# Four steps of h in a row, then x Wx of two pairs: regrouping a recurrent layer on one core of a Trainium2

## The chip, the cores and the metric

The kernel runs on one core of a Trainium2 chip. The metric is the time of the device in microseconds for one execution of the whole program. The engines are called as in the profile: PE is TensorE's matmul and PEld its weight load, DVE is VectorE, ACT is ScalarE, POOL is GpSimd, SP is SyncE, from which nearly all transfers are issued.

## The reference

There are 64 sequences of 256 steps with 1024 features. The first layer is a recurrence over the 256 steps; the second multiplies by a gate that depends on the sequence alone.

```python
def step(prev_h, xw):
    next_h = jnp.tanh(prev_h @ Wh + xw)
    return (next_h, next_h)
xW = jnp.einsum('ntd,dh->nth', x, Wx) + b
...
_, h_t = jax.lax.scan(step, h0, xW_t)
x = x + jnp.swapaxes(h_t, 0, 1)
...
h = jax.nn.silu(q_pool @ W1.T + b1)
gate = jax.nn.sigmoid(h @ W2.T + b2)[:, None, :]
...
return v + a
x = x + _L1_cond_ref(x, cond_1024, W1, b1, W2, b2)
```

The Haar transform is linear and the gate is the same for all its levels, so its result is v times the gate. With v + a and the outer addition, the second layer becomes a multiplication of (x + h) by a factor 2 + gate.

## The kernel before, in words

**Steps and pairs.** Two steps are a pair (S = 2), so there are 128 pairs (NP); x of a pair is one slab of 128 x 1024 in fp32, step and sequence interleaved in its free dimension. Six slabs exist. The product x Wx doesn't depend on h and is made for a whole pair; the product of h has to wait for the step before.

**The product of h.** A step multiplies h (64 x 1024) by Wh in full fp32 with one level of Strassen's scheme: seven half-size products (`strassen_product`, L190), each of 16 matmuls in the code, 32 matmuls and 32 weight loads in the trace. Their order in the loop is 1, 4, 2, 5, 6, 7, 3. The four quarters of h are finished as their products come in: DVE adds (L710, L725, L731), ACT takes the tanh (L685), DVE transposes the quarter to hT (L689). L720 adds two operands that both lie in SBUF. After the last quarter, DVE makes four sums of quarters for the next step (`strassen_sides`, L225 to L228). ACT puts the next step's x Wx in three PSUM banks, into which products of h accumulate (`put_part`, L607; called by `put_next`).

**The product of x.** x is split into a high and a low part[...]: x0 (the high bits, cast by ACT, L309), x1 (x - high, L298), and x2, a combination of both for the mixed terms (L303). `XWork.whole` (L331) issues 16 mixed matmuls, then 16 main ones with x1 and 16 with x0. `take_mixed` evacuates the mixed product with ACT and adds b with POOL (L319, L320); `finish_half` adds the main product with DVE (L374). The sum of a pair goes to DRAM and comes back as two tiles by step (`store` L384, `reload` L392, eight transfers). The tiles high, x0, x1, x2 and sum have one buffer each; xw has three.

**The loop.** From step ALONE = 12 on, the order on all engines is that of the program. Each pair of steps is followed by `beside_x`: the product of x for the pair two ahead (`now`), the addition of h to both steps of x by POOL (L645), the multiplication by the factor by POOL (`scale`, L494), the split of the pair three ahead (`nxt`), and the store of the finished pair. PE thus runs two steps of h (14 products), one pair of x (48 matmuls of 128 x 512), two steps of h, and so on. Steps before 12 are made with other code that the change hardly touches; they leave five pairs in DRAM (`kept`) that are multiplied by the factor later. The last x product comes after step 251; steps 252 to 255 follow each other without one. The last step is stored in a layout of its own (`times_factor`, `plus_x`).

**SP's queue.** Within `beside_x` it holds the store of the last sum (made to wait for `mark`, the copy of u in the step, so that transfers keep out of the products of h), the load of a slab, the reloads of that sum, and the store of the slab finished one pair earlier.

Of the kernel before, what the change touches and what calls it, by code (L numbers as in the profile page):

```python
# [51 lines left out]
F32 = mybir.dt.float32  # L53
# [16 lines left out]
S = 2  # L70
NP = T // S
# [12 lines left out]
def tile_cond_resid(  # L84
# [197 lines left out]
    class XWork:  # L282
# [17 lines left out]
        def difference(self) -> None:  # L300
            i = self.i
            self.x2 = split.tile([P, D], F32R, tag="x2", name=f"x2_{i}")
            nc.vector.scalar_tensor_tensor(  # L303
                out=self.x2, in0=self.x1[:].bitcast(F32), scalar=-UP, in1=self.high, op0=ALU.mult, op1=ALU.add
            )
# [195 lines left out]
    for t in range(ALONE):  # L501
# [56 lines left out]
        if LATE <= t < LATE + B:  # L558
# [6 lines left out]
            if k == B - 1:  # L565
                factor, factor_n = gate_factor(b2_n), b2_n
# [7 lines left out]
        if s == S - 1:  # L574
            del pairs[i]
            load_x(i + 3)
# [22 lines left out]
    load_x(i + 3)  # L599
# [9 lines left out]

    def not_ahead_of(dma, ins) -> None:  # L610
# [7 lines left out]
    leaving = []  # L618

    def store_y() -> None:  # L620
        while leaving:
            j = leaving.pop()
            nc.sync.dma_start(out=yT[j], in_=pairs.pop(j))

    def transfers(i: int, mark) -> None:

        if mark and i + 1 < NP - 1:
# [4 lines left out]
        if mark and i + 1 < NP - 1:  # L632
            xws[i + 1] = later.reload(d)
        store_y()

    def beside_x(t: int, steps: list, mark):

        i = t // S
        x = pairs[i]
        transfers(i, mark)  # L640
        now = coming
        if now:
            now.whole()
        for r, v in steps:
            nc.gpsimd.tensor_add(of_step(x, r), of_step(x, r), blocks(v))  # L645
# [24 lines left out]
    coming.cast()  # L670
    later, coming = beside_x(t, [(s, hT)], None)
    x_n = None
    for t in range(ALONE, T):
        i, s = divmod(t, S)
        final = t == T - 1
        xw, before = xws[i][s], hT
# [28 lines left out]
        if s == 0 and coming is not None:  # L705
# [11 lines left out]
        put_next(0) if s == 0 else None  # L717
# [4 lines left out]
        put_next(2) if s == 0 else None  # L722
# [41 lines left out]
        if t >= 2 * B and t % 2 == 1 and kept:  # L764
            j, r = divmod((t - 1) // 8 - B // 4, S)

            def at(v):
                return v.rearrange("p (b s n) -> p s b n", b=B, s=S)[:, r]

            if t % 8 == 1:  # L770
                again = const.tile([P, W], F32, tag="spare", name=f"again{t}")
                by_block = again[:].rearrange("p (b n) -> p b n", b=B)
                nc.sync.dma_start(out=by_block, in_=at(kept[j]))
            elif t % 8 == 3:
                v = again[:].rearrange("p (b g m) -> p g b m", b=B, g=G)
                nc.gpsimd.tensor_mul(v, v, blocks(factor))
            elif t % 8 == 5:
                nc.sync.dma_start(out=at(yT[j]), in_=by_block)
                if (j + 1, r + 1) == (len(kept), S):
                    kept = []  # L780
# [34 lines left out]
```

## Time and profile before

| what | value |
| --- | --- |
| median of 3 runs | 3047.43 us (3046.83 to 3047.49) |
| the profiled execution, whole | 3048.26 us |
| its span | 3046.5 us |
| granted clock of PE | 1.00 |
| main matmuls of x, L274 | 4064; 32 in 7.25 us by the chain of waits |
| mixed matmuls of x, L274 | 2032 |
| additions of h to x by POOL, L645 | 243, mean 1389 ns |
| multiplications by the factor by POOL, L494 | 244, mean 1772 ns |
| one such addition by DVE, L748 | 684 ns |
| DVE sum of quarters L226 and L227 | mean 311 and 813 ns |

The durations of matmuls in the profile overlap (a product of h is listed with 32 records of 273 ns and passes in 0.87 us), so they are read from start to start, or from the chain of waits, which lists the pieces of PE's stream one behind the other. In the timeline a bracket behind an instruction gives the idle time of its engine before it and what ended it.

### The profile page before, as it was taken

What the parts mean: (1) busy time and instruction counts of PE and PEld (TensorE: products, weight loads), DVE (VectorE), ACT (ScalarE), POOL (GpSimd) and SP (SyncE); (2) the same over time, 40 slices, a digit from 0 to 9 for tenths busy, and PEclk for the clock granted to TensorE, in tenths of its full rate; (3) what the DMA queues carried; (4) which work ended last, traced back from release to release, by engine and by line L of the source; (5) the groups of instructions that cost most, each with busy time, mean ns of one, the idle gap of its engine ahead of it and who ended that gap; (6) DMA issues with size and microseconds to landing.
All of it is one profiled execution on the core that took longest, in us unless ns stands there. A gap on an engine that the chain in (4) does not pass through costs nothing.

```text
span 3046.5 us, 141663 instructions
## 1 busy us (share of the span) xinstructions
PE 3036.6 (100%) x63862; PEld 2708.3 (89%) x63862; DVE 2028.4 (67%) x4683; ACT 868.6 (29%) x2641; POOL 1176.9 (39%) x766
## 2 busy tenths in 40 slices
PE   9999999999999999999999999999999999999999
PEld 6888899888988998889888998899888988898888
DVE  7566666666666666666666666666666666666666
ACT  3222232222222222222222222232222222222222
POOL 2224433443344433433343334433443334333432
PEclk9999999999999999999999999999999999999999
DMA  7323322332233223222222223222322232222222
GB/s 264 125 82 100 100 93 94 106 101 89 93 104 105 93 89 103 99 86 86 96 95 93 86 91 98 95 86 87 102 96 85 86 101 98 86 89 99 100 85 79
DMA packets 164605, 300.40 MB, mean 99 GB/s; under 512 B 44192, under 2 KB 110496, under 8 KB 164000
## 3 DMA queue, kind: packets, MB, share of 16 engines
q1 hardware_dynamic: 163856, 290.81, 28.7%
q8 instruction: 501, 8.21, 1.1%
q14 instruction: 104, 0.85, 0.1%
q10 hardware_dynamic: 144, 0.52, 0.1%
HBM read 154.93 MB, written 136.31 MB: 96 GB/s over the span
## 4 chain that ended last, share of the span: by engine, by line
PE 99%; POOL 0%; DMA 0%; DVE 0%; issue 0%; SPq 0%; ACT 0%; DVEq 0%; ACTq 0%
PE main L274 30%; PE acc L195 22%; PE mixed L274 16%; PE m_h L195 15%; PE main_h L195 14%; PE m L195 1%; PE acc L212 0%; PE gate_ps L212 0%; POOL sum L320 0%; DMA wx<-wx 0%; PE acc_raw L212 0%; DVE x L298 0%; SPq L406 0%; DVE sum L374 0%; ACT acc L607 0%
## 5 line engine op out<-in xcount | busy, mean ns | idle before, releaser
L645 POOL TENSOR_TENSOR x<-x,hT 128x512 f32<-128x512 f32 x243 | 333.1, 1389 | 1714.4 <-DVE hT L689 1696.5
L274 PE MATMUL main<-wx,x 128*128 128x512 f32 x4064 | 945.7, 389 | 0.8 <-DVE x L298 0.8
L274 PEld LDWEIGHTS main<-wx,x 128*128 128x128 f32 x4064 | 762.1, 188 | 161.6 <-issue 2.2
L274 PE MATMUL mixed<-wx,x 128*128 128x512 f32 x2032 | 499.3, 397 | 0.0
L274 PEld LDWEIGHTS mixed<-wx,x 128*128 128x128 f32 x2032 | 371.8, 188 | 98.0 <-issue 24.8
L685 ACT ACTIVATE h<-h 128x128 f32<-128x128 f32 x976 | 275.6, 306 | 553.2 <-DVE h L710 333.2
L494 POOL TENSOR_TENSOR x<-x,factor 128x512 f32<-128x512 f32 x244 | 427.4, 1772 | 5.8 <-DVE factor L480 5.7
L320 POOL TENSOR_TENSOR sum<-sum,b_row 128x512 f32<-128x512 f32 x254 | 383.5, 1530 | 57.4 <-ACT sum L319 50.4
L298 DVE TENSOR_TENSOR x<-x,x_high 128x1024 fp32r<-128x1024 f32 x127 | 212.3, 1672 | 230.7 <-PE main L274 230.6
L689 DVE STREAM_TRANSPOSE hT<-h 128x128 f32<-128x128 f32 x972 | 297.7, 306 | 38.7 <-ACT h L685 38.5
L710 DVE TENSOR_TENSOR h<-acc,y 128x128 f32<-128x128 f32 x244 | 71.1, 292 | 333.7 <-PE acc L195 333.7
L195 PE MATMUL acc<-wh,s 128*32 128x128 f32 x8160 | 273.9, 273 | 0.0
L195 PE MATMUL acc<-t,hT 128*32 128x128 f32 x8160 | 270.3, 273 | 0.6 <-ACT acc L607 0.4
L195 PE MATMUL acc<-wh,hT 128*32 128x128 f32 x8160 | 270.2, 273 | 0.0
L195 PE MATMUL main_h<-wh,s 128*32 128x128 f32 x7808 | 261.9, 273 | 0.6 <-issue 0.6
L195 PE MATMUL m_h<-t,s 128*32 128x128 f32 x7808 | 261.0, 273 | 0.4 <-issue 0.4
L195 PE MATMUL m_h<-wh,hT 128*32 128x128 f32 x7808 | 261.2, 274 | 0.0
L704 ACT COPY y<-m_h 128x128 f32<-128x128 f32 x244 | 65.1, 267 | 684.5 <-PE m_h L195 669.2
L195 PE MATMUL main_h<-t,s 128*32 128x128 f32 x7808 | 259.4, 273 | 0.1
L607 ACT COPY acc<-xw 128x128 f32<-128x128 f32 x732 | 177.7, 264 | 257.0 <-DMA xw<-sum_d 187.3
L195 PEld LDWEIGHTS m_h<-wh,hT 128*32 128x32 f32 x7808 | 208.6, 110 | 42.8 <-issue 42.8
L319 ACT ACTIVATE sum<-mixed 128x512 f32<-128x512 f32 x254 | 149.8, 598 | 321.6 <-PE mixed L274 215.8
(81 smaller groups left out, 3418.7 us busy)
## 6 DMA issues: line engine op xcount, KB each, us to landing
x<-xT SPq DMA_DIRECT2D x127, 512.0 KB, 5.2
sum_d<-sum SPq DMA_DIRECT2D x127, 512.0 KB, 3.2
xw<-sum_d SPq DMA_DIRECT2D x1016, 64.0 KB, 2.0
yT<-x SPq DMA_DIRECT2D x122, 512.0 KB, 2.7
wh<-wh SPq DMA_DIRECT2D x8, 512.0 KB, 10.8
w<-w1T SPq DMA_DIRECT2D x8, 512.0 KB, 8.7
w<-w2T SPq DMA_DIRECT2D x8, 512.0 KB, 4.2
wx<-wx SPq DMA_DIRECT2D x7, 512.0 KB, 8.7
```

Source lines behind the costliest of these rows:

```text
L195: nc.tensor.matmul(out=out[q * R : (q + 1) * R], lhsT=a[:, k * R : (k + 1) * R], rhs=wh_s.sides[i][k][:, q], start=first and k == 0, stop= ...
L274: nc.tensor.matmul(out=acc[h], lhsT=v[:, k * P : (k + 1) * P], rhs=wx_s[k][which][:, h * HALF : (h + 1) * HALF], start=start and k == 0, s ...
L298: nc.vector.tensor_sub(self.x1, x, self.high)
L319: nc.scalar.activation(s, self.mixed[h], AF.Copy, scale=-DOWN)
L320: nc.gpsimd.tensor_add(s, s, b_row[:, h * HALF : (h + 1) * HALF])
L494: nc.gpsimd.tensor_mul(of_step(x, s), of_step(x, s), blocks(factor))
L607: nc.scalar.copy(part, xws[t // S][t % S][:, j])
L645: nc.gpsimd.tensor_add(of_step(x, r), of_step(x, r), blocks(v))
L685: nc.scalar.activation(quad(h, j), quad(h, j), AF.Tanh)
L689: nc.vector.transpose(quad(hT, j), quad(h, j))
L704: nc.scalar.copy(y[:, 0], m16)
L710: nc.vector.tensor_add(quad(h, 0), accs[0], y[:, 0])
```

## The change

The program works in groups of M = 4 steps. Products of h of four steps follow each other; then `beside_x` issues the products of x for two pairs, `one` (which was split during the x products before) and `two` (split while `one` is multiplied, from the slab loaded one group earlier), and splits a third pair, `three`, for the next group's `one`. x2 is made from high and x instead of from high and x1, with another scale, which `take_mixed` takes into account; so it is made ahead of x1. The addition of h to x is done by DVE in each step (`residual`), right after the sums of quarters, or, for the last step of a group, ahead of the splits. POOL keeps the multiplications by the factor and the addition of b. Four xw tiles are needed by group: the fourth lies in a constant tile that is free by then. `put_next` runs in the first three steps of a group; for the first step of a group, the three banks are filled during the x products. The kept pairs and the last step's x are handled in the same rhythm, and in the last group DVE does the multiplications of the three steps before the last.

```diff
@@ -68,6 +69,7 @@
...
 S = 2
+M = 4
 NP = T // S
@@ -301,7 +303,7 @@
...
             nc.vector.scalar_tensor_tensor(
-                out=self.x2, in0=self.x1[:].bitcast(F32), scalar=-UP, in1=self.high, op0=ALU.mult, op1=ALU.add
+                out=self.x2, in0=self.high, scalar=1.0 + DOWN, in1=pairs[i], op0=ALU.mult, op1=ALU.subtract
             )
@@ -316,7 +318,7 @@
...
                 s = self.sum[:, h * HALF : (h + 1) * HALF]
-                nc.scalar.activation(s, self.mixed[h], AF.Copy, scale=-DOWN)
+                nc.scalar.activation(s, self.mixed[h], AF.Copy, scale=-1.0)
                 nc.gpsimd.tensor_add(s, s, b_row[:, h * HALF : (h + 1) * HALF])
@@ -383,11 +385,16 @@
...
-        def reload(self, d) -> list:
+        def reload(self, d, late: bool = False) -> list:
             d = d[:].rearrange("(s g m) (q f) -> s q m g f", s=S, g=G, q=Q)
...
             for s in range(S):
-                t = xwpool.tile([P, 4, E], F32, tag="xw", name=f"xw{self.i * S + s}")
+                name = f"xw{self.i * S + s}"
+                if late and self.i * S % M + s == M - 1:
+                    t = const.tile([P, 4, E], F32, tag="h0T", name=name)
+                else:
+                    t = xwpool.tile([P, 4, E], F32, tag="xw", name=name)
                 for q in range(Q):
@@ -563,7 +570,7 @@
...
             if k == B - 1:
-                factor, factor_n = gate_factor(b2_n), b2_n
+                factor = gate_factor(b2_n)
         if t + 1 == ALONE:
@@ -573,6 +580,7 @@
...
             del pairs[i]
+        if s == S - 1 or t + 2 == ALONE:
             load_x(i + 3)
@@ -596,7 +604,6 @@
...
     xws = {ALONE // S: xw_next}
-    load_x(i + 3)
@@ -606,6 +613,10 @@
...
         return part
+    def residual(t: int, hT) -> None:
+        v = x_step(t)
+        nc.vector.tensor_add(v, v, blocks(hT))
@@ -615,65 +626,98 @@
...
-    leaving = []
-    def store_y() -> None:
-        while leaving:
-            j = leaving.pop()
-            nc.sync.dma_start(out=yT[j], in_=pairs.pop(j))
-    def transfers(i: int, mark) -> None:
-        if mark and i + 1 < NP - 1:
+    def store_y(i: int) -> None:
+        nc.sync.dma_start(out=yT[i], in_=pairs.pop(i))
+    def beside_x(t: int, mark):
+        i = t // S
+        steps = [(i - 1, 0), (i - 1, 1), (i, 0), (i, 1)] if mark else [(i, 1)]
+        if mark:
             d, dma = later.store()
...
             load_x(i + 4)
-        if mark and i + 1 < NP - 1:
-            xws[i + 1] = later.reload(d)
-        store_y()
-    def beside_x(t: int, steps: list, mark):
-        i = t // S
-        x = pairs[i]
-        transfers(i, mark)
-        now = coming
-        if now:
-            now.whole()
-        for r, v in steps:
-            nc.gpsimd.tensor_add(of_step(x, r), of_step(x, r), blocks(v))
-        if now:
-            now.take_mixed()
-        for r, _ in reversed(steps):
-            scale(x, r)
-        leaving.append(i)
-        nxt = None
+        if mark:
+            xws[i + 1] = later.reload(d, True)
+        one = coming
+        one.whole()
+        residual(t, hT)
+        for j, r in steps[:2]:
+            scale(pairs[j], r)
+        if mark:
+            store_y(i - 1)
+        if i + 5 < NP:
+            load_x(i + 5)
+        elif i + 4 < NP:
+            ends.append(slab("ends"))
+            nc.sync.dma_start(out=ends[0][:, :W], in_=xN)
+        one.take_mixed()
+        if mark:
+            accs[:] = [put_part(t + 1, j) for j in range(3)]
+        two = three = None
         if i + 3 < NP:
-            nxt = XWork(i + 3)
-            nxt.low()
-        if now:
-            now.finish_half(0)
-        if nxt:
-            nxt.difference()
-        if now:
-            now.finish_half(1)
-        if i + 2 >= NP - 1:
-            store_y()
-        if i + 2 == NP - 1:
-            xws[i + 2] = now.relay()
-        return now, nxt
+            two = XWork(i + 3)
+            two.difference()
+            two.low()
+        else:
+            x_n, factor_n = ends[0][:, :W], ends[0][:, W:]
+            nc.vector.transpose(factor_n, factor)
+            nc.vector.tensor_mul(x_n, x_n, factor_n)
+        one.finish_half(0)
+        one.finish_half(1)
+        for j, r in steps[2:]:
+            scale(pairs[j], r)
+        kept_step(t)
+        d, _ = one.store()
+        store_y(i)
+        xws[i + 2] = one.reload(d, True)
+        if two:
+            two.cast()
+            two.whole()
+            two.take_mixed()
+        if i + 4 < NP:
+            three = XWork(i + 4)
+            three.difference()
+            three.low()
+        if two:
+            two.finish_half(0)
+            two.finish_half(1)
+        return two, three
+    again = []
+    def kept_step(t: int) -> None:
+        n, odd = divmod(t // M - ALONE // M, 2)
...
     accs = [put_part(ALONE, j) for j in range(3)]
-    coming = later
+    coming, later, ends = later, None, []
     coming.cast()
-    later, coming = beside_x(t, [(s, hT)], None)
-    x_n = None
+    later, coming = beside_x(t, None)
     for t in range(ALONE, T):
...
         final = t == T - 1
-        xw, before = xws[i][s], hT
+        last_of_group = t % M == M - 1
+        xw = xws[i][s]
         m16, m5, m7 = (bank(tag, f"{tag}_h{t}")[:, :E] for tag in ("m16", "main0", "main1"))
@@ -689,20 +733,19 @@
...
         def put_next(j: int) -> None:
-            if not final:
+            if not last_of_group:
                 nxt[j] = put_part(t + 1, j)
...
         def times_factor(v: slice) -> None:
-            nc.vector.tensor_mul(h[:, v], h[:, v], factor_n[:, v])
+            nc.vector.tensor_mul(h[:, v], h[:, v], ends[0][:, W + v.start : W + v.stop])
         def plus_x(v: slice) -> None:
-            nc.vector.tensor_add(h[:, v], h[:, v], x_n[:, v])
+            nc.vector.tensor_add(h[:, v], h[:, v], ends[0][:, v])
             nc.sync.dma_start(out=yT[i][:, W + v.start : W + v.stop], in_=h[:, v])
...
         nc.scalar.copy(y[:, 0], m16)
-        if s == 0 and coming is not None:
+        if t % M == 0 and coming is not None:
             coming.cast()
@@ -714,12 +757,17 @@
...
             plus_x(slice(0, E))
-        put_next(0) if s == 0 else None
+        elif t > T - M:
+            v = x_step(t - 1)
+            nc.vector.tensor_mul(v, v, blocks(factor)) if t < T - 1 else None
+            store_y(i - 1) if t == T - S else None
+        put_next(0)
         strassen_product(m16, sides[6], 6)
...
         nc.vector.tensor_add(y[:, 2], accs[2], u)
-        put_next(2) if s == 0 else None
+        put_next(2)
         strassen_product(m7, sides[7], 7, True)
@@ -737,47 +785,20 @@
...
         transpose(2)
-        put_next(1) if s == 0 else None
+        put_next(1)
         transpose(1)
         sides = strassen_sides(hT, t)
+        accs = nxt
         if t == T - 2:
...
             last = slab("last")
-            v = of_step(pairs[i], s)
-            nc.vector.tensor_add(v, v, blocks(hT))
-            nc.vector.tensor_mul(blocks(last[:, :W]), v, blocks(factor))
+            residual(t, hT)
+            nc.vector.tensor_mul(blocks(last[:, :W]), x_step(t), blocks(factor))
             nc.sync.dma_start(out=yT[i][:, :W], in_=last[:, :W])
-        if s == 1:
-            later, coming = beside_x(t, [(1, hT), (0, before)], mark)
-            for o in range(3):
-                put_next(o)
-        accs = nxt
-        if t == T - 4 * B - 1:
-            x_n = const.tile([P, W], F32, tag="spare", name="x_n")
-            nc.sync.dma_start(out=x_n, in_=xN)
-        if t == T - 4 * B + 1:
-            nc.vector.tensor_scalar_add(factor_n, factor_n, 2.0)
-            nc.vector.tensor_mul(x_n, x_n, factor_n)
...
+        elif last_of_group:
+            later, coming = beside_x(t, mark)
+        else:
+            residual(t, hT)
```

More of the change, by code (lines that the diff above doesn't have):

```diff
@@ new lines, in beside_x, with at @@
+        return two, three
+    again = []
+    def kept_step(t: int) -> None:
+        n, odd = divmod(t // M - ALONE // M, 2)
+        def at(v, n: int):
+            return v[n // S].rearrange("p (b s n) -> p s b n", b=B, s=S)[:, n % S]
+        if not 0 <= n <= S * len(kept):
+            return
+        if odd and again:
+            v = again[0][:].rearrange("p (b g m) -> p g b m", b=B, g=G)
+            nc.gpsimd.tensor_mul(v, v, blocks(factor))
+        if not odd:
+            if again:
+                v = again.pop()[:].rearrange("p (b n) -> p b n", b=B)
+                nc.sync.dma_start(out=at(yT, n - 1), in_=v)
+            if n < S * len(kept):
+                again.append(const.tile([P, W], F32, tag="spare", name=f"again{n}"))
+                v = again[0][:].rearrange("p (b n) -> p b n", b=B)
+                nc.sync.dma_start(out=v, in_=at(kept, n))
@@ L739, in tile_cond_resid @@
         transpose(2)
-        put_next(1) if s == 0 else None
+        put_next(1)
         transpose(1)
         sides = strassen_sides(hT, t)
+        accs = nxt
         if t == T - 2:
             last = slab("last")
-            v = of_step(pairs[i], s)
-            nc.vector.tensor_add(v, v, blocks(hT))
-            nc.vector.tensor_mul(blocks(last[:, :W]), v, blocks(factor))
+            residual(t, hT)
+            nc.vector.tensor_mul(blocks(last[:, :W]), x_step(t), blocks(factor))
             nc.sync.dma_start(out=yT[i][:, :W], in_=last[:, :W])
-        if s == 1:
-            later, coming = beside_x(t, [(1, hT), (0, before)], mark)
-            for o in range(3):
-                put_next(o)
-        accs = nxt
-        if t == T - 4 * B - 1:
-            x_n = const.tile([P, W], F32, tag="spare", name="x_n")
-            nc.sync.dma_start(out=x_n, in_=xN)
-        if t == T - 4 * B + 1:
-            nc.vector.tensor_scalar_add(factor_n, factor_n, 2.0)
-            nc.vector.tensor_mul(x_n, x_n, factor_n)
[L764 to L780, printed above, removed]
+        elif last_of_group:
+            later, coming = beside_x(t, mark)
+        else:
+            residual(t, hT)
 def kernel(x, cond_1024, L0_cond_Wx, L0_cond_Wh, L0_cond_b, L1_cond_W1, L1_cond_b1, L1_cond_W2, L1_cond_b2):
```

## The prediction

> **What bounds the kernel now.** I read the page first (busy shares, chain, queues), then the chain of waits in windows in the middle of the loop, then the timeline of the same windows, and last the end of the run, where four steps already follow each other without x products between them.
>
> ```profile
> span 3046.5 us, 141663 instructions
> PE 3036.6 (100%) x63862; PEld 2708.3 (89%) x63862; DVE 2028.4 (67%) x4683; ACT 868.6 (29%) x2641; POOL 1176.9 (39%) x766
> ...
> q8 instruction: 501, 8.21, 1.1%
> ...
> PE 99%; POOL 0%; DMA 0%; DVE 0%; issue 0%; SPq 0%; ACT 0%; DVEq 0%; ACTq 0%
> ```
>
> The reader is to see that TensorE's own order sets the end: 99% of the chain is PE. Only three things can move the time: how many products there are (the change leaves them alone), what a switch between kinds of products costs, and gaps on PE. The chain of waits over one pair of steps prices the switch:
>
> ```profile
> 1515.16 0.87 PE m_h L195 x32
> 1516.03 1.75 PE acc L195 x64
> ...
> 1521.27 3.85 PE mixed L274 x16
> 1525.12 7.25 PE main L274 x32
> 1532.38 1.01 PE m_h L195 x32
> 1533.39 1.75 PE acc L195 x64
> ```
>
> A product of h in the stream takes 0.87 us, the first after x 1.01: 0.14 more. 32 matmuls of x take 7.25, so 16 should take 3.63; the first 16 after h take 3.85: 0.22 more. So one h-to-x-to-h pair of switches costs 0.36 us. The step s=1 (from 1515.16) follows s=0 with no gap.
>
> The same chain where it is not smooth:
>
> ```profile
> 738.70 0.61 PE acc L195 x22
> 739.31 0.18 issue
> 739.49 1.39 PE acc L195 x41
> ...
> 743.18 0.28 issue
> 743.47 0.52 PE main_h L195 x10
> ```
>
> Here PE stops in mid-product, waiting for no semaphore ("issue"). I took the starts of all such stops in h from the trace. Before the last four steps there are 19, in 17 of the 120 runs of h products; each ends at the same count of PE records modulo 256 (193 or 194), 2.3 to 2.9 us after the start of the last 16 KB packet on q8 (739.49 after 737.20, 743.47 after 740.65). So they are waits for a page of instructions. They hold the weight loads 0.07 to 0.55 us and lie 7.4 to 12.1 us into a run of h products, none earlier.
>
> The timeline shows what room VectorE has in a step:
>
> ```profile
> 1516.82 0.29 DVE L228 TENSOR_TENSOR s<-hT,s 128x128 f32<-128x128 f32 x1
> 1517.92 0.29 DVE L710 TENSOR_TENSOR h<-acc,y 128x128 f32<-128x128 f32 x1 [0.80 <-PE acc L195]
> 1519.89 0.29 DVE L720 TENSOR_TENSOR y<-y,u 128x128 f32<-128x128 f32 x1 [0.66 <-ACT u L719]
> ...
> 1522.40 2.75 POOL L645 TENSOR_TENSOR x<-x,hT 128x512 f32<-128x512 f32 x2 [14.24 <-DVE hT L689]
> 1522.61 1.38 DVE L227 TENSOR_TENSOR s<-s,hT 128x128 f32<-128x128 f32 x1
> ```
>
> [...] early in a run of h, the packet starts 0.25 of a page (64 of 256 records) earlier against the products than after a stop[...] L227 takes 1.38 us beside L645, and 0.28 elsewhere (739.13)[...].
>
> **The change part by part.**
>
> *Fewer switches.* Before, x products run 121 times (after t = 11, 13 ... 251), each for one pair; after, 61 times (11, 15 ... 251), all but the last for two. 60 pairs of switches go: 60 x 0.36 = **21.6 us off**, all on the chain.
>
> *Longer runs of h.* 120 runs of two steps become 60 of four; the last one of four is there before too. A product is 64 PE records (32 loads, 32 matmuls) in 0.873 us, so a page of 256 lasts 3.49 us. From the packets of q8: within runs of h the next packet starts 3.75 us (121 cases, first to second) and 3.72 us (115, second to third) after the one before, not 3.49; the packet takes 1.10 us, the wait after a stop shows some 1.4 us from landing to use and 1.2 from use of one page to the next packet: 3.7 together. So in a run of h each page loses about 0.26 us, paid from the lead of 64 records = 0.87 us, which x products (0.23 us a matmul, so 96 records in 11.1 us) refill. A run of two steps has 14 x 64 / 256 = 3.5 pages, of which on average 3 have their boundary and their successor inside: 3 x 0.26 = 0.78, under 0.87, so a stop only in some runs. That fits: mean length of the runs 12.43 us, usual 12.36, 0.06 a run. A run of four steps has 7 pages, 6.5 counted so: 6.5 x 0.26 = 1.69, less 0.87, is 0.82; packets scatter (0.9 to 1.45 us) and a run cannot gain below nothing, so I take **0.85 us a run**. Sum: 60 x 0.85 = 51.0, less what the 120 short runs lose now, 120 x 0.06 = 7.4: **43.6 us on**. Bounds: a page at 3.65 us gives 6.5 x 0.16 - 0.87 = 0.17 a run, 2.8 us in all; the seven packets in the last four steps start at 3016.30 to 3040.72, 4.07 us each, or 3.91 without the 0.97 us that PE there waits for data: 6.5 x 0.42 - 0.87 = 1.86 a run, 104 us.
>
> *Residual on VectorE.* 243 additions leave POOL (L645, 1389 ns); the added one is L748's form, 684 ns. In the step it comes after L228 and before L710, where VectorE waits 0.80: it fits with 0.1 to spare, and L710 may be 0.1 late, which its transpose (needed 1.7 us later by the next step's first product) absorbs: 0. Behind it in VectorE's queue wait L710, L712 and the transposes; were that cover gone, 0.3 us a step. In the last step of a group it lies beside x.
>
> *Scaling.* POOL's multiplication of the earlier pair (L494; 1.28 us unhindered at 1528.10) no longer follows POOL's own addition in x. It can start as soon as the residual on VectorE is done, thus inside the second and third step of the group. There it lies between about 2.7 and 4.0 us after the step's start; the next VectorE instruction with two SBUF inputs is L720 at 4.7. Cost 0. If both multiplications come together in one step, the second meets L720; the end of the run shows the price:
>
> ```profile
> 3031.44 2.52 POOL L494 TENSOR_TENSOR x<-x,factor 128x512 f32<-128x512 f32 x2
> ...
> 3032.88 1.22 DVE L720 TENSOR_TENSOR y<-y,u 128x128 f32<-128x128 f32 x1 [0.42 <-ACT u L719]
> ...
> 3034.59 0.38 PEld L195 LDWEIGHTS m_h<-wh,hT 128*32 128x32 f32 x16 [0.16 <-issue]
> 3035.25 0.81 PEld L195 LDWEIGHTS acc<-t,hT 128*32 128x32 f32 x32 [0.28 <-DVE hT L689]
> ```
>
> L720 0.93 late, and PE loses up to 0.44.
>
> *Second split and transfers.* Per x stretch of about 22 us VectorE does two splits (1.56 + 1.45 + 1.67 each) and four finishes (0.68): 12.1 us, in room of 22. x2 now needs high and x alone, so it can follow the mixed products (3.85 us in); x1 follows the main x1 products (7.5 in), x0's cast (1.05 on ACT) the end at 11.1, needed at 18.5. ACT's evacuation of the second pair waits for the first sum's store (done near 12, 3.2 to landing), 15.5, and the addition by POOL is done by 19.5, before VectorE's finish at 20.4. SP's queue holds two stores, two loads, sixteen reloads (0.57 each) and two y stores: the second reload ends near 23, used first two steps later. The load behind the first y store waits for its landing (2.7), with the next 512 KB not needed before the following stretch. No wait of PE: 0.
>
> *The end.* At t = 253 the old order held back the evacuation copies (0.41 of PE), and POOL met L720 (up to 0.44). Both go, though the page waits take part of that back: **0.7 off**.
>
> Sum: 43.6 - 21.6 - 0.7 = +21.3. The profiled execution took 3048.26 (1.76 outside its span); it would take 3069.6. The median of the runs is 0.83 lower: **3069 us**.
>
> **The rivals.** *A, likeliest, 60%:* as worked out, 3053 to 3100. *B, faster, 17%:* the wait for pages in a run of four steps stays near what two short runs lose (0.12 together). Place: boundaries in steps three and four; price: 21.6 and 0.7 off, 3025; at 0.17 a run 3028. It decides below 0.12 + 0.36 = 0.48 us a run. For it: 103 of the 120 short runs have no stop, and transfers in h get rarer. Against it: the packets fall behind steadily, and stops come only late in a run, and the last four steps have three such stops, 11.8, 19.7 and 23.5 us in. *C, balance, 13%:* 0.4 to 0.58 a run, within 0.2% (6 us, about what a measurement of this kernel tells from no change), 3047. *D, slower, 10%:* collisions of POOL's scaling with L720, twice in each group at 0.44: 60 x 0.88 = 53, less 22.3, 3078. Against it is the early start of the scaling; and with PE late for pages, part of it would be hidden.
>
> **How the numbers follow.** Faster is B, 0.17; same C, 0.13; slower A and D, 0.70. Range: A's upper bound with 1.3 us a run gives 60 x 1.3 - 7.4 - 22.3 = +48; D on top of some of A lies near +50; downward half of B's chance must be taken in with C. I take 3035 to 3098; A alone would be 3055 to 3090.
>
> **What would show it.** In the chain of the changed kernel, 1.01 and 3.85 appear once per 28 products: else the first term is wrong. Pieces named "issue" in steps three and four, about 0.85 us a run of four steps (24.6 us without): 0.1 means B. A wait of PE on ACT or DVE at L720's late end means D. L710 after the residual at its old place in the step confirms the cost of nothing for it. The forecast fails if pages arrive every 3.6 us or less in long runs.

## The result, and the profile after

The changed kernel takes 3050.65 us (median of 20 runs, 3044.25 to 3057.76), the kernel before 3046.25 us beside it (20 runs, 3045.17 to 3048.18). The ratio is 1.0015, with a 95% interval from 1.0008 to 1.0022: +4.4 us, small but clear of the noise, where +21.3 us were forecast. The profiled execution took 3049.05 us, 0.8 more than the one before; the analysis below is of this pair, and the other 3.6 us of the medians are in executions without a trace. So this is a large rearrangement that moved the time hardly at all, and the question is where its two large terms went.

The page of the changed kernel, header, queue of instructions and shares of the chain:

```profile
span 3047.2 us, 141801 instructions
...
PE 3029.6 (99%) x63862; PEld 2716.6 (89%) x63862; DVE 1791.4 (59%) x4928; ACT 866.9 (28%) x2641; POOL 808.3 (27%) x521
...
q8 instruction: 501, 8.21, 1.1%
...
PE 99%; issue 0%; POOL 0%; DMA 0%; DVE 0%; SPq 0%; ACT 0%; DVEq 0%
```

PE has the same 63862 matmuls and still makes 99% of the chain; POOL has 245 instructions fewer, DVE 245 more. "issue" rounds to 0% here but now stands right behind PE. PE is busy 7.0 us less in a span that is 0.7 us longer: something was saved, and something else was put in its place.

The chain of waits over one group of four steps and the x products behind it (start, duration, what):

```profile
1663.16 1.01 PE m_h L197 x32
1664.17 1.75 PE acc L197 x64
...
1680.14 0.32 issue
1680.46 0.96 PE main_h L197 x27
...
1688.58 3.85 PE mixed L276 x16
1692.43 7.25 PE main L276 x32
1699.69 3.63 PE mixed L276 x16
1703.32 7.25 PE main L276 x32
1710.57 1.01 PE m_h L197 x32
```

The dear first pieces, 1.01 and 3.85, appear once per 28 products; the second pair of x passes at 3.63, so nothing is lost inside the double stretch. The price is in the middle: PE stops for 0.32 us at 1680.14, 17 us into the run, with no semaphore to wait for.

The stops by engine and tile, from the view of waits (total us, times, longest); after, and below it before:

```profile
PEld m_h L197 <- issue: 29.1, 79, 0.7
...
PEld acc L197 <- issue: 13.0, 32, 1.0
PEld mixed L276 <- issue: 12.9, 65, 0.2
...
PEld main_h L197 <- issue: 6.2, 17, 0.6
```

```profile
PEld m_h L195 <- issue: 44.3, 126, 0.6
...
PEld mixed L274 <- issue: 24.8, 125, 0.2
```

The "mixed" line is the switch to x: 125 times 0.2 before, 65 after. The "m_h" line of before is nearly all the switch back (one per run); after, it mixes that switch with real stops, and "acc" and "main_h", 1.2 and 2.4 us in the view of before, are almost all stops. Taken one by one from the trace, the changed kernel has 88 such stops with 27.6 us in all, in 42 of its 61 runs of h. Every one ends where the count of PE records is 193 or 194 modulo 256, and only 3 of the 88 lie in the first 12 us of a run. I read them as waits for a page of instructions, 256 records to one packet on q8: the 501 packets carry 8.21 MB, 16 KB each, and 501 x 256 is 128,256, 0.4% above the 127,724 records of PE and PEld.

I measured every run of h from its first product to the first x product, and every x stretch likewise, in both traces. A run of four steps without a stop takes 24.59 us (the shortest of the 60 that have x products behind them), one of two steps 12.364.

| where | forecast, us | found, us | how found |
| --- | --- | --- | --- |
| switches | -21.6 | -21.3 | x stretches 1343.8 to 1330.8, and 60 x (24.59 - 2 x 12.364) in h |
| page waits in the runs of h of the loop | +43.6 | +21.9 | 60 runs lose 0.482 us each (28.95), 120 short runs lost 7.08 |
| last four steps | -0.7 | -0.8 | 26.40 to 25.65 us, to the start of the last matmul |
| start of the loop's first x product | 0 | +1.4 | 180.06 to 181.44 us |
| behind the start of the last matmul | 0 | -0.5 | 5.42 to 4.95 us |
| sum, in the span | +21.3 | +0.7 | 3046.5 to 3047.2 |

The same trace ties the loss of a run to its pages. Between the 60 runs, the loss and the mean spacing of the packets on q8 go together (correlation 0.90): the 30 runs with the closest packets (3.60 us on average) lost 0.15 us each, the other 30 (3.79 us) 0.82. A stop may also put off the next packet (in this trace the next one starts 1.2 us behind a stop's end at the median), so this shows the tie and not its direction, for which the places of the stops and the experiments are needed.

### The profile page after: what moved, and what is told of

Its sections match the earlier page's. It is cut to its first block, busy times and chain, and to the rows that moved or that the text cites. A ratio compares the mean times of both kernels' runs of the same rounds, so it can differ in the third digit from the quotient of the medians.

```text
span 3047.2 us, 141801 instructions
## 1 busy us (share of the span) xinstructions
PE 3029.6 (99%) x63862; PEld 2716.6 (89%) x63862; DVE 1791.4 (59%) x4928; ACT 866.9 (28%) x2641; POOL 808.3 (27%) x521
## 3 DMA queue, kind: packets, MB, share of 16 engines
q8 instruction: 501, 8.21, 1.1%
## 4 chain that ended last, share of the span: by engine, by line
PE 99%; issue 0%; POOL 0%; DMA 0%; DVE 0%; SPq 0%; ACT 0%; DVEq 0%
PE main L276 30%; PE acc L197 22%; PE mixed L276 16%; PE m_h L197 14%; PE main_h L197 14%; PE m L197 1%; PE acc L214 0%; PE gate_ps L214 0%; POOL sum L322 0%; DMA wx<-wx 0%; PE acc_raw L214 0%; DVE x L300 0%; SPq L413 0%; ACT sum L321 0%; SPq L119 0%
## 5 line engine op out<-in xcount | busy, mean ns | idle before, releaser
L322 POOL TENSOR_TENSOR sum<-sum,b_row 128x512 f32<-128x512 f32 x254 | 409.9, 1626 | 1119.0 <-ACT sum L321 1109.4
L501 POOL TENSOR_TENSOR x<-x,factor 128x512 f32<-128x512 f32 x242 | 368.2, 1531 | 1007.0 <-issue 561.4
L300 DVE TENSOR_TENSOR x<-x,x_high 128x1024 fp32r<-128x1024 f32 x127 | 176.9, 1393 | 269.8 <-PE main L276 269.7
L376 DVE SCALAR_TENSOR_TENSOR sum<-main,sum 128x512 f32<-128x512 f32 x254 | 175.4, 691 | 203.1 <-PE main L276 181.4
L197 PE MATMUL acc<-wh,s 128*32 128x128 f32 x8160 | 282.6, 273 | 1.3 <-issue 1.0
L197 PE MATMUL acc<-wh,hT 128*32 128x128 f32 x8160 | 279.5, 273 | 1.6 <-issue 1.3
L197 PE MATMUL main_h<-t,s 128*32 128x128 f32 x7808 | 269.2, 273 | 1.2 <-issue 0.8
L305 DVE SCALAR_TENSOR_TENSOR x<-x_high,x 128x1024 fp32r<-128x1024 f32 x127 | 174.5, 1374 | 155.3 <-PE mixed L276 155.2
L197 PEld LDWEIGHTS acc<-wh,s 128*32 128x32 f32 x8160 | 238.0, 110 | 4.3 <-issue 4.1
L197 PEld LDWEIGHTS m_h<-wh,hT 128*32 128x32 f32 x7808 | 217.8, 110 | 26.3 <-issue 25.9
```

Of the source, the lines that this page charges most:

```text
L197: nc.tensor.matmul(out=out[q * R : (q + 1) * R], lhsT=a[:, k * R : (k + 1) * R], rhs=wh_s.sides[i][k][:, q], start=first and k == 0, stop= ...
L300: nc.vector.tensor_sub(self.x1, x, self.high)
L305: nc.vector.scalar_tensor_tensor(out=self.x2, in0=self.high, scalar=1.0 + DOWN, in1=pairs[i], op0=ALU.mult, op1=ALU.subtract)
L376: nc.vector.scalar_tensor_tensor(out=v, in0=self.main[h], scalar=1.0 + DOWN, in1=v, op0=ALU.mult, op1=ALU.add)
L501: nc.gpsimd.tensor_mul(of_step(x, s), of_step(x, s), blocks(factor))
```

## The experiments

Theory P: PE outruns its supply of instructions in a run of h. Each page arrives some 0.2 us later than it is used up (3.69 us from packet to packet, 3.49 for 256 records in the products' time), a lead (0.87 us, the prediction's estimate from the 64 records that it read in the trace of before) covers the first pages, and what a run loses depends on its length and on the spacing of the packets on q8, on no other engine. Rival D: part of the time comes from data (the residual on VectorE, POOL's scaling meeting L768, the old L720). Rival T: the transfers delay the pages, so the losses come from where the DMAs lie. A "ratio" is to the kernel before, with its 95% interval. The runs were made in four groups, each on another chip, so each is compared with the kernel before that ran beside it: 3044.74 us for e1, e3, e4 and e5; 3044.26 for e2, e2b, e4b and e7; 3043.12 for a_after_again, e5c, e8 and e8b; 3043.84 for a_after_third, e2_runs_alone_again and e9.

### The residual alone, and without it

The first of these takes the kernel before and lets VectorE add h to x within the step; the second takes the changed kernel and gives the addition back to POOL.

```diff
-        for r, v in steps:
-            nc.gpsimd.tensor_add(of_step(x, r), of_step(x, r), blocks(v))
+        r, v = steps[0]
+        nc.vector.tensor_add(of_step(x, r), of_step(x, r), blocks(v))
...
+        elif s == 0:
+            v = of_step(pairs[i], s)
+            nc.vector.tensor_add(v, v, blocks(hT))
```

> The kernel before with one part of the change alone: h is added to x by VectorE right after the sums of quarters in each step, no longer by POOL; runs of two steps as before. Theory (pages of instructions and switches decide): PE does not wait for it, within 2 us of the kernel before. Rival (the residual on VectorE delays the steps): 0.1 us a step or more, 24 us slower.

Measured: 3044.31 us (13 runs), ratio 1.0 [0.9992, 1.0008]; runs of two steps 12.397 us on average, x stretches 11.105.

```diff
     def residual(t: int, hT) -> None:
         v = x_step(t)
-        nc.vector.tensor_add(v, v, blocks(hT))
+        (nc.vector if t == T - 2 else nc.gpsimd).tensor_add(v, v, blocks(hT))
```

> The changed kernel with one part undone: h is added to x by POOL (1.3 us) in each step, just before the multiplications by the factor. Theory (pages hold the runs): POOL's instruction meets the sums of quarters and L710 waits behind them; the runs have slack from the late pages, 0 to 10 us slower. Rival (moving the addition to VectorE is what makes long runs possible): over 0.1 us a step, more than 24 us slower.

Measured: 3044.75 us (13 runs), ratio 1.0002 [0.9994, 1.001]; runs 25.045 us, 88 stops with 24.4 us at the page's place in the count of records, none for data. POOL's addition does meet the sums of quarters here (L229 takes 1206 ns on average), and PE still doesn't wait. The unaltered changed kernel did not run on that chip; on three others its mean run was 24.90 to 25.08 us, and within that spread the engine of the residual is worth nothing in either arrangement. So rival D falls. The groups of the changed kernel's profile say the same (operations, then busy us and mean ns, then idle time before):

```profile
L619 DVE TENSOR_TENSOR x<-x,hT 128x512 f32<-128x512 f32 x244 | 167.1, 685 | 0.0
...
L229 DVE TENSOR_TENSOR s<-s,hT 128x128 f32<-128x128 f32 x255 | 75.8, 297 | 0.0
...
L768 DVE TENSOR_TENSOR y<-y,u 128x128 f32<-128x128 f32 x244 | 71.3, 292 | 163.5 <-ACT u L767 163.3
```

L229, the old L227, falls from 813 to 297 ns with POOL's addition gone from beside it, and rises to 1206 where the addition is given back to POOL. L768 at 292 ns shows no meeting with POOL's scaling; the timeline shows how it is avoided:

```profile
1671.28 0.69 DVE L619 TENSOR_TENSOR x<-x,hT 128x512 f32<-128x512 f32 x1
...
1672.10 1.29 POOL L501 TENSOR_TENSOR x<-x,factor 128x512 f32<-128x512 f32 x1 [11.55 <-issue]
...
1672.17 0.29 DVE L753 TENSOR_TENSOR h<-acc,y 128x128 f32<-128x128 f32 x1 [0.20 <-PE acc L197]
...
1674.14 0.29 DVE L768 TENSOR_TENSOR y<-y,u 128x128 f32<-128x128 f32 x1 [0.66 <-ACT u L767]
```

VectorE is through with the residual 0.20 us before L753 may start, and POOL's multiplication ends at 1673.39, 0.75 before L768. L753, beside that multiplication, still takes 0.29: from 180 us on, 120 of its 244 executions overlap an instruction of POOL's, and these take 292 ns on average like the other 124. It has an operand in PSUM; L768 has both in SBUF, and took 1.22 us beside POOL in the prediction's view of the end (there L720).

### PE alone

This kernel computes nothing of the layer: PE issues products of h, in runs of 14 to 56, each behind 48 matmuls in the shape of x's, with no wait on another engine, and at the end runs whose matmuls are twice as wide.

```python
for r in range(14):
    for n in (14, 21, 28, 42, 56):
        x_part()
        for _ in range(n):
            product(m, E)
for r in range(6):
    x_part()
    for _ in range(28):
        product(wide, F)
```

> Nothing of the reference is computed but the products themselves: PE alone issues runs of 14, 21, 28, 42 and 56 products of h's shape, without a wait for any other engine, each behind 48 matmuls of x's shape, 14 times over, and then six runs of 28 products twice as wide. Theory (3.69 us a page against 3.49, lead 0.87): stops a run of 0.05, 0.2, 0.5, 1.1 and 1.8 us, and none in the wide runs, which need a page in 7 us. Rival (data of other engines, or transfers beside the runs): no stops at any length.

> PE alone in runs of 14 to 56 products of h's shape, as before, on the chip of this batch; nothing else of the reference is computed. Theory: a page each 3.60 to 3.70 us in the long runs, as 3.64 before, and stops in runs of 28 of 0.1 to 0.3 us. If this chip has slow pages, the changed kernel's mean run is longer too.

Mean loss of a run above the shortest possible, in us:

| products in the run | 14 | 21 | 28 | 42 | 56 |
| --- | --- | --- | --- | --- | --- |
| first chip | 0.00 | 0.02 | 0.14 | 0.46 | 1.26 |
| another chip | 0.03 | 0.09 | 0.15 | 0.51 | 0.99 |

The packets came every 3.64 and 3.63 us in the long runs, closer than in the kernels here. Waits of the first of the two:

```profile
PEld m L134 <- issue: 53.4, 152, 0.6
...
PEld x L147 <- issue: 14.9, 70, 0.4
...
PEld wide L134 <- issue: 2.1, 6, 0.4
```

With no other engine at work PE still stops (70 of the 152 are the switch), and the loss grows faster than the length of the run, as a lead that is used up would make it. The wide runs have the same number of instructions in twice the time and lose nothing: 48.484 us every time, six waits for six switches. So P's mechanism needs neither data nor transfers. The size was over-expected: for 28 products 0.5 us was expected, while 6.5 pages at 3.64 us, 0.15 above 3.49, less 0.87 of lead give an estimate of 0.11, near the 0.14 found. That is also less than a third of the 0.48 in the changed kernel.

The same with 512 KB loads and stores going on all the while:

```diff
+    for j in range(240):
+        t = slabs.tile([P, D], F32, tag="traffic", bufs=2, name=f"traffic{j}")
+        nc.sync.dma_start(out=t, in_=xT[j % NP])
+        nc.sync.dma_start(out=yT[j % NP], in_=t)
```

> The same runs, with 512 KB loads from and stores to DRAM going on all the time. Theory: the round trip of a page hardly depends on transfers (packets take 1.05 us beside x and 1.10 in h): stops within 30% of those of the quiet runs. Rival (pages are late because of transfers): several times as long.

The transfers ended near 955 us of 3217, which the slices of the page show (busy tenths of the DMA engines, and GB/s):

```profile
DMA  7777777777760000000000000000000000000000
GB/s 279 270 277 266 269 269 269 268 273 268 269 232 4 3 4 3 3 4 3 4 4 3 4 3 3 4 3 4 3 4 3 3 4 3 3 3 2 2 2 9
```

While they went on, runs of 28 lost 1.06 to 3.96 us each; afterwards 0 to 0.2. The packets came every 3.95 us instead of 3.62, although a packet itself took 1.07 us as ever. So my expectation for it (stops within 30% of the quiet ones) failed, and rival T is right for this kernel: with such traffic beside the runs, a page came 0.33 us later. In the changed kernel, transfers beside the runs are not the cause: its traffic lies beside the x products, with about 33 KB in the first 3 us of a run and next to nothing from there to its last 0.6 us. The packets in its runs came every 3.69 us, and the 321 of 333 intervals between them with less than 2 KB of traffic also average 3.69.

### More instructions in the run

Two NoOps ahead of each product of the loop shorten the page in products (3.88 instead of 4).

```diff
     def strassen_product(out, a, i: int, first: bool = False) -> None:
+        for _ in range(nop_now[0]):
+            nc.tensor.nop(hint="pad", nofuse=True)
...
+        nop_now[0] = 2
         strassen_product(m16, sides[1], 1, True)
```

> The changed kernel with two empty instructions (NoOp) on TensorE's queue ahead of each product of h, 56 in a run of four steps (0.22 of a page). Theory (pages arrive every 3.7 us in a run): a run needs 0.22 x 3.69 = 0.8 us more where it is already held by pages, 0.6 to 0.8 on average, so 35 to 50 us slower than the changed kernel (3050.65). Rival (the longer runs wait for data of other engines): no more than a few us.

Measured: 3154.34 us, ratio 1.0357 [1.0343, 1.0371]; runs 26.77 us, 1.69 more than the 25.08 of the changed kernel's first trace, where 0.6 to 0.8 were expected; all 61 runs have stops, about 250 of them at the page's place, with some 110 us; x stretches unchanged at 22.00. The direction is P's, the size is not. The records of NoOps in a row start about 74 ns apart (below), which would be 4.1 us for the 56 of a run, so they may add time of their own as well as records to the page. It supports P but measures nothing cleanly.

### Where the page boundary falls

A group of the changed kernel takes 53 instructions less than eight pages, so the boundary wanders through the runs. With 53 NoOps per group it stays at one place. I put them behind 8 matmuls of the first of the two pairs, and chose with a larger number in the first stretch the boundary 24 records into the run (first kernel), or 128 (second).

```diff
             for h in range(2):
                 for k in range(B):
                     x_matmul(self.mixed, self.x2, 2, h, k, True, True)
+                if h == 0:
+                    for _ in range(53 if self.i % 2 and self.i > 7 else 72 if self.i == 7 else 0):
+                        nc.tensor.nop(hint="pad", nofuse=True)
```

> The changed kernel with 53 NoOps in each x stretch, after its first eight matmuls, and none in h. A group then has 2048 PE records, 8 pages, and the first page boundary of each run of h lies 24 records after its start. Theory: NoOps beside x cost nothing[...]; and a boundary just behind the start lets the next page arrive during x, so that five of the boundaries have to be paid for instead of six: about 0.2 us a run less, 10 us faster than the changed kernel. Rival (data): as the changed kernel, within 3 us.

> The changed kernel with 53 NoOps in each x stretch as before, but with 152 more in the first, so that the first boundary of each run lies 128 records after its start. Theory: six boundaries to be paid for in every run: as the changed kernel or up to 5 us slower, and 10 to 14 us slower than with the boundary at 24. Rival (NoOps in x help or harm by themselves): the same time as with the boundary at 24.

Measured: 3255.08 us, ratio 1.0694 [1.0674, 1.0713], and 3157.16 us, ratio 1.037 [1.0356, 1.0385]. The first was expected to be 10 us faster than the changed kernel, the second as fast or up to 5 us slower; they rose by 210 and 113 us above the kernel before. The chain of the first:

```profile
1187.54 2.04 PE mixed L276 x8
1189.57 1.41 issue
1190.98 2.06 PE mixed L276 x8
...
1236.57 2.05 PE mixed L276 x8
1238.62 2.36 issue
1240.98 3.65 PE mixed L276 x8
```

The eight matmuls ahead don't cover the NoOps, whose records in the trace start 74 to 76 ns apart on average: PE stands for 1.4 to 2.4 us here, and in 1240.98 eight matmuls take 3.65 instead of about 1.8, at a granted clock of 0.53 in that piece (0.977 over the whole span). In 43 of the 60 double stretches of this trace the granted clock is 0.5 for 3.4 us, behind a standstill of 1.9 to 2.8 us; these take 26.14 us on average, the other 17 take 24.08. In the second kernel, with the same NoOps at the same place, every standstill but the first is 1.2 to 1.3 us, with no granted clock of 0.5 behind it, and the stretch takes 23.52 us. So the NoOps cost some 1.5 us a stretch; the rest of the first kernel's loss comes from longer standstills and the lower clock. Its page boundary lies among the NoOps, the second's 104 records later; that this makes the standstill longer is likely, but no run tests it alone. In the runs of h, which are clean of NoOps, the boundary at 24 gave 24.812 us a run and at 128 gave 25.10, the unaltered kernel 25.082: 0.27 better at 24, where 0.2 were expected. These are three chips, and the unaltered kernel's own mean run differs by up to 0.18 between chips.

So the NoOps were moved behind 24 matmuls, the rest as above:

```diff
                 for k in range(B):
                     x_matmul(self.main, self.x1, 1, h, k, start=True)
+                if h == 0:
+                    for _ in range(53 if self.i % 2 and self.i > 7 else 72 if self.i == 7 else 0):
+                        nc.tensor.nop(hint="pad", nofuse=True)
```

> The changed kernel with 53 NoOps in each x stretch, now after 24 of its matmuls instead of 8, first page boundary 24 records into each run of h. With the NoOps after 8 matmuls the runs took 24.81 us on average (unaltered 25.08), but the x stretch 25.55 (21.99). Theory: a NoOp takes TensorE's sequencer about 62 ns (53 take 3.3 us), 8 matmuls cover 1.8 us of it, 24 cover all, and no boundary lies among the NoOps any more: x stretch 22.0, runs 24.8, so 16 us faster than the changed kernel, some 12 us faster than the kernel before. Rival (NoOps stop TensorE wherever they stand): x stretch 23.5 or more, 90 us slower.

> As the one before, but the first boundary 128 records into each run. Theory: runs as in the unaltered kernel (25.1), so 0 to 3 us off the changed kernel, and 16 us slower than with the boundary at 24: the place of the boundaries alone makes the difference. Rival (NoOps themselves help): as fast as with 24.

Measured: 3036.75 us (16 runs), ratio 0.9979 [0.9972, 0.9987], with runs of 24.797 and x of 22.10 us; and 3053.2 us, ratio 1.0039 [1.0027, 1.0052], with runs of 24.975 and x of 22.01 but for the first. That one carries 224 NoOps, whose records take 16.5 us (74 ns each, where 62 were expected, about what 1.5 us lost in a stretch above and 1.8 of the eight matmuls make for 53); PE stands for 12.3 us, the granted clock is 0.5 for 13.7 (0.997 over the whole span), and the stretch takes 36.27 us instead of 22.0. Without these 14.3 us the second kernel would stand near 3039 (an estimate). The first kernel's stretch and runs came out nearly as expected, the gain did not: it is 6.4 us faster than the kernel before, where some 12 were expected, and 2.3 faster than the changed kernel of the same chip (below: 3039.09 us, runs of 24.899), where 16 were. The boundary at 24 took 0.10 us off a run there and not 0.2, and the x stretch gave 0.1 back. The second kernel is 14.1 us slower than the changed one, where 0 to 3 were expected, and its first stretch is all of that.

The same for the kernel before, with 27 NoOps in each stretch, which brings the boundary 192 to 193 records into each run of two steps, behind 8 matmuls (not 16, as the expectation of the second has it) and behind 24:

```diff
+                if h == 0:
+                    for _ in range(27 if self.i > 7 else 0):
+                        nc.tensor.nop(hint="pad", nofuse=True)
```

> The kernel before with 27 NoOps in each x stretch: a pair of steps then has 1024 PE records, 4 pages, and the first boundary lies 192 records into each run of two steps. Theory: three boundaries in a run, of which two have to be paid for, below the lead of 0.87 us; stops fall from 0.06 us a run to 0.01: 5 to 7 us faster than the kernel before. Rival: no change.

> The kernel before with 27 NoOps in each x stretch, after 24 of its matmuls instead of 16, boundary 192 records into each run of two steps. Theory: as with the earlier place, runs of 12.37 us instead of 12.42 or 12.40: 3 to 6 us faster than the kernel before.

Measured: 3043.39 us, ratio 0.9997 [0.9988, 1.0005], and 3041.63 us, ratio 0.9995 [0.9987, 1.0004]. The traces show the expected shift (the mean run falls from 12.423 us to 12.375 and 12.369, and the stops that are left lie 9.6 to 9.8 us into a run), but the gains, 1.4 and 1.5 us where 5 to 7 and 3 to 6 were expected, are within the intervals: a faster kernel is not shown.

### The same kernel on other chips

> The changed kernel, unaltered, beside the others of this batch and the kernel before: 1 to 6 us slower than before by the 20 runs already made (ratio 1.0008 to 1.0022). With POOL adding h to x it was within 0.1% of before; if both are alike here, that part of the change is worth nothing either way.

> The changed kernel, unaltered, once more. Theory: its time beside the kernel before follows from the mean run of four steps in its trace: 25.08 us gave +4.4 us against before, 24.90 gave -4.0, so each 0.02 us of the mean run is worth about 1 us here; a mean of 24.99 would be a tie. Rival (another term changes from chip to chip): no such relation.

The unaltered changed kernel: 3039.09 us (21 runs), ratio 0.9986 [0.998, 0.9993], and on a further chip 3041.13 us, ratio 0.9991 [0.9984, 0.9997]. That is 4.0 and 2.7 us faster than the kernel before beside it, where it was 4.4 slower at first; 1 to 6 us slower had been expected for the first of these. The three profiled executions tell what differs:

| profiled execution, us | mean run of h | all stops in runs of h, sum | packets every | first x of the loop at |
| --- | --- | --- | --- | --- |
| 3049.05 | 25.082 | 27.7 | 3.693 | 181.44 |
| 3038.89 | 24.899 | 15.8 | 3.658 | 182.56 |
| 3043.29 | 25.003 | 22.8 | 3.686 | 180.51 |

Between the first two, 61 x 0.183 = 11.2, less 1.1 for the later start, is about 10.0, and 10.16 was measured; between the first and the third, 61 x 0.079 = 4.8 (from 1530.0 and 1525.2 us) and 0.9 for the start give 5.7, with 5.76 measured. So what differs between these three executions is how promptly pages came: the stops differ by 11.9 and 4.9 us, like the runs. That the sign of the medians follows from it is argued, for there is one traced execution per chip. By the expectation for the third, 24.99 us would be a tie with the kernel before; its trace has 25.003, and its own time is 0.6 us below that kernel's 3043.84, but the median of its 21 executions is 2.7 below.

### The version that beats both

The NoOps in the second pair's products, where 72 of the 96 matmuls lie ahead of them; boundary 24 records into the run.

```diff
+                if h == 0:
+                    for _ in range(0 if self.i % 2 else 53 if self.i > 8 else 72):
+                        nc.tensor.nop(hint="pad", nofuse=True)
```

> The changed kernel with 53 NoOps in each x stretch after 72 of its 96 matmuls, first boundary 24 records into each run of h. Where they stood after 24 matmuls, the x stretch was still 0.1 us longer (22.10 for 21.99) and the runs 0.1 to 0.2 shorter (24.80). Theory: [...] x stretch 22.0, runs 24.8: 6 us faster than the changed kernel of this batch, or more where its runs are longer than 24.9. Rival (the boundary's place is worth nothing): within 2 us of it.

Measured: 3035.05 us (7 runs), ratio 0.997 [0.9959, 0.9981]: 8.8 us faster than the kernel before, and 6.1 faster than the changed kernel on that chip (3041.13); their intervals, up to 0.9981 and from 0.9984, don't meet. 6 us faster than the changed kernel was expected. The x stretches take 22.012 us, so here the NoOps are hidden (their records again start 73 ns apart). The profile comes from the slowest of the seven, at 3040.68: its runs of h took 24.932 us against 25.003. Of the median execution there is no trace, so that the rest of its gain also comes from the runs is not shown.

## Why the prediction was right and wrong

- **Fewer switches: right.** 21.3 us went, where 21.6 were forecast from four rows of one chain.
- **Longer runs of h: the mechanism right, the size wrong.** This is the step that failed. It took 0.85 us a run; the trace has 0.482, and the traces from the two other chips have 0.30 and 0.41. The term of its sum that was mis-sized is the loss of a page: 0.26 us, from packets every 3.75 us, the higher of the two values that the trace of before showed, where the changed kernel's came every 3.69, a loss of 0.20. With that, the step's own formula, 6.5 x 0.20 less 0.87, gives 0.43. Its own sign of failure, pages every 3.6 us or less, did not come. A difference of 0.06 us in a packet's spacing is multiplied by 6.5 pages, and since the formula subtracts a fixed 0.87 us it halves what remains. The prediction's lower bound of 3.65 us (0.17 a run) and the upper one (1.86) show how steep this is; it didn't draw the consequence that its likeliest case could not be so much likelier than its neighbours. A slip beside this is small: 120 x 0.06 is 7.2, not 7.4, and the short runs lost 7.1.
- **The rivals.** The account that came true is C, balance: 0.4 to 0.58 us a run. The point of decision, 0.48, held: at 0.482 the loop lost as much as it gained. B's reason, that 103 of 120 short runs have no stop, was no evidence for long ones, and A's, that packets fall behind steadily, was right (3.69 us against 3.49); only its size was too large. D didn't happen.
- **Residual and scaling at nothing: right.** Both placements of the residual measure the same, and the scaling ended before L768, as worked out.
- **Second split and transfers at nothing: right.** No stop of PE in the x stretches is for data: the double stretch took 21.994 us on average, and 3.85 + 7.25 + 3.63 + 7.25, with no gap, is 21.98.
- **The end: right**, -0.8 for -0.7, and its last run still lost 1.26 us to pages (25.65 us, against 24.39 for the same stretch of a run without a stop). Not foreseen were the +1.4 us ahead of the loop. They are two page stops in the first twelve steps, in code that the kernel before has too: up to 180 us both traces have the same products in the same order, and the changed kernel, 0.2 us ahead until then, falls back by 1.0 us at 89.5 and by 0.6 at 102.7. In its second trace the same two stops are longer, in its third shorter. The -0.5 us behind the last matmul, also not foreseen, I did not separate; it and the +1.4 us in part cancel.

What stays open is why the packets' spacing differs between executions, chips and kernels without traffic (3.63 to 3.73 us). It matters: by the formula, the 0.06 us between PE alone and the changed kernel is 0.4 us a run, most of its loss. No run tried that, nor runs of three steps.

## What to carry to other kernels

When PE's own stream is the bound, price the supply of instructions like any buffer: the time that PE needs for 256 records (3.49 us here), against the spacing of the packets on the instruction queue (3.63 to 3.73 us without traffic), and the length of the dense stretch. A gain that rests on joining dense stretches should be forecast as a difference of two like numbers, with the range that the spread of the packets makes. Measure such a change on more than one chip, for here its sign changed between them.

## What was not expected of the hardware

- With 512 KB loads and stores beside the runs, PE alone had its packets every 3.95 us against 3.62 afterwards, while a packet took 1.07 us as ever. Without transfers, its runs of up to 21 products lost 0.09 us or less on average, and those with matmuls twice as wide nothing.
- NoOps on PE are not free: their records start 73 to 76 ns apart. 53 of them are hidden behind 72 matmuls (22.012 against 21.99 us), nearly behind 24 (22.10), and not behind 8 (1.2 to 2.8 us of standstill).
- Standstills of 1.9 to 2.8 us were followed by 3.4 us at a granted clock of 0.5, in 43 of 60 stretches of one trace; among the other 17 are standstills of 1.4 to 2.65 us, so the length alone doesn't decide. None followed those of 1.2 to 1.3 us.
- The changed kernel's own time scatters over 13.5 us in 20 executions, the kernel before over 3.0. In the three that were traced, the differences are those of the page stops; for the rest it is an inference.
